# Inner sums over two slices, and stores that wait for GpSimd moved some slots back, in a masked graph attention kernel

## The chip, the cores and the metric

The kernel runs on one core of a Trainium2 chip. The metric is the device time of one execution in microseconds. A core has TensorE (matmuls, PE in the profile; its weight loads are PEld), VectorE (DVE), ScalarE (ACT), GpSimd (POOL) and SyncE (SP), whose queue issues nearly all DMAs of this kernel. Each engine works through its own instructions in their order, and so does SyncE's queue: an instruction that waits holds up all that stand behind it on its engine.

## What is computed

128 graphs of 128 nodes with 768 features go through one layer of attention with a normalization in front, 12 heads of 64, all in float32:

```python
h = jnp.maximum(_layernorm(x, axis=-1), 0.0)
q = _split_heads(h @ Wq + bq)
k = _split_heads(h @ Wk + bk)
v = _split_heads(h @ Wv + bv)
scores = jnp.einsum('bhqd,bhkd->bhqk', q, k) / jnp.sqrt(HD)
scores = scores + beta * adj_e
scores = jnp.where(adj_e > 0, scores, -9e15)
probs = jax.nn.softmax(scores, axis=-1)
x = x + einsum('bhqk,bhkd->bhqd', probs, v)   # heads put back together
```

The adjacency is non-zero in about one place of eight.

## The kernel before

**Groups and slices.** Four graphs make a group, and there are 32 groups. A group's projections come in three slices: `qk0` (queries and keys of heads 0 to 5), `v` (all heads), `qk1` (queries and keys of heads 6 to 11). A slice multiplies activations of 2 x 3 blocks (`A00` to `A12`) by weights of 3 x 3 blocks (`B00` to `B22`). Instead of 18 block products it takes the 15 of a fast scheme (`PRODUCTS`, line 66): sums of activation blocks (`S0` to `S14`, `SUMS_A`) meet sums of weight blocks (`T0` to `T13`, `SUMS_B`), and results are added up with signs.

**Two kinds of product.** `product` (line 564, slice `qk1`) takes a block product as it is, with its weight sums kept in SBUF. `product_z` (line 488, slices `qk0` and `v` from group 1 on) splits each block product once more in two by two and takes seven small products for eight. That needs four more subtractions or additions of 128x128 for each activation sum, made on GpSimd by `inner` (line 420) into `spbuf`, and a prepared weight tile of seven parts, of 448 KB. The 30 prepared tiles lie in DRAM (`kept`); `load_T` (line 298) brings them, one for each product, into a ring of five. A `product_z` issues the load of the tile five places on behind its own matmuls. GpSimd also undoes the scheme behind each finished result: `decode` (line 537).

**The first group.** The prepared tiles don't exist yet. Group 0 takes `qk0` and `v` by `plain_slice` (line 767), 18 units in which plain block products are added up in PSUM, while `prepare` (line 245) makes the 30 tiles step by step: sums on VectorE, four subtractions on GpSimd (`rest` or `finish`), then a store. Its `qk1` is taken with 15 products.

**Slots.** The order of the work is written out by hand. A slice has 15 slots (18 in `plain_slice`), one for each product. `then(at, f, ...)` puts a step into slot `at`, behind that product's matmuls and before its results are read out; `(at, "post")` puts it at the slot's end. `later(f, n)` puts off a step to the n-th slot's end from here on (1 is this one), over the slices' ends if need be; `overdue` runs those that are due. All engines get their instructions in this order.

**What runs beside the products** of group G: scores of heads 6 to 11 of the group before in `qk0` and of heads 0 to 5 of G in `v`, in slots 1 and 2; `attend` (probabilities times values, three in `qk0`, three in `qk1`), woven between the matmuls by `turn`; behind each of them `weigh` (quotients, VectorE and ScalarE), an addition to the input on GpSimd (`add`, line 661) and a store of 256 KB (`send`, line 664). For the groups to come: normalization and transposes in `v` and `qk1`, `sum_acts` (VectorE) and `inner` (GpSimd) of G + 1 in `qk1`, row statistics of G + 2 on VectorE (`row_stats`), whose moments (`row_moments`, line 383) are two small operations on GpSimd, a store to DRAM (line 395) and a load that spreads them over the partitions (line 396); the adjacency and x of G + 2 are loaded by SyncE too. `activations` (line 942) holds the slots of the sums; all but one of the sums and 14 of the 15 `inner` steps of G + 1 lie in `qk1` of G, in slots 3 to 14, the last ones in slots 0 and 1 of `qk0`.

Of the kernel before, what the change touches and what calls it, by code (L numbers as in the profile page):

```python
# [10 lines left out]
F32 = mybir.dt.float32  # L11
# [6 lines left out]
P = 128  # L18
# [96 lines left out]
def direct(ctx, tc, x, adj, wq, bq, wk, bk, wv, bv, beta, out, bad):  # L115
# [129 lines left out]
    def prepare(sl):  # L245
# [4 lines left out]
        def rest(n, t):  # L250
            e = nc.gpsimd
            e.tensor_tensor(t[:, 2], t[:, 4], t[:, 1], ALU.subtract)
# [16 lines left out]
        def finish(name):  # L269
            n = [i for i, p in enumerate(PRODUCTS) if p[1] == name][0]  # L270
            if name in made:
                rest(n, made[name])
            else:
                t, b = home(n), wt[sl, name]
                e = nc.gpsimd
                for z, c, i in ((0, 0, 0), (3, 1, 0), (4, 1, 1)):
                    nc.scalar.copy(t[:, z], b[:, c, i])
                e.tensor_tensor(t[:, 2], b[:, 1, 1], b[:, 0, 1], ALU.subtract)
                e.tensor_tensor(t[:, 6], b[:, 0, 1], b[:, 0, 0], ALU.subtract)
                e.tensor_tensor(t[:, 1], t[:, 4], t[:, 6], ALU.subtract)  # L280
                e.tensor_tensor(t[:, 5], t[:, 3], t[:, 1], ALU.subtract)
                k = kept[sl, n] = dram.tile([P, 7, P], F32, name=f"kept_{sl}_{n}")
                nc.sync.dma_start(k, t)
# [99 lines left out]
    def row_moments(G):  # L383
# [11 lines left out]
        nc.sync.dma_start(turned.rearrange("i b s -> b i s"), t.rearrange("p s g -> p (s g)"))  # L395
        nc.sync.dma_start(to.rearrange("p b s g -> p (b s g)"),
                          turned.rearrange("i b s -> i (b s)")[None].to_broadcast([NB, SQ, NB * 2 * GRP]))
# [245 lines left out]
    def attend_steps(G, oc):  # L643
# [24 lines left out]
        later(send, 3)  # L668
# [98 lines left out]
    def plain_slice(G, sl, todo):  # L767

        n = 0
        for r in range(2):  # L770
            for j in range(3):
# [3 lines left out]
                parts = (slice(0, N), slice(N, H2)) if sl != "v" and r == j == 0 else (slice(0, H2),)  # L775
                for at, k in [(at, k) for at in parts for k in range(3)]:
                    a, b = A[G, f"A{r}{k}"], wt[sl, f"B{k}{j}"]
                    for i in range(2):
                        for c in range(2):
                            lhs, rhs = b[:, c, i], a[:, c, at]  # L780
                            if sl == "v":
                                lhs, rhs = a[:, c, i * N:(i + 1) * N], b[:, c].rearrange("p i n -> p (i n)")
                            last = nc.tensor.matmul(p[:, i, at], lhs, rhs, start=(k == 0 and i == 0 and c == 0),
                                                    stop=(c == 1), skip_group_check=True)
# [20 lines left out]
                    for f in todo.get(n, ()):  # L805
                        f()
                    overdue()
                    n += 1
# [133 lines left out]
    def activations(G, first):  # L942

        for name, at in (("A01", 3), ("A00", 5), ("A02", 6), ("A11", 9), ("A10", 17), ("A12", 24)):
            if at >= 15:
                then(at - 15, to_hT, G, int(name[1]), int(name[2]))
            elif first:
                then(0, to_hT, G, int(name[1]), int(name[2]))
# [6 lines left out]
    raw_qk(1, const.tile([P, NC * VH * 2], F32, name="wqk1"), ((0, 3),))  # L955
# [10 lines left out]
    for r in range(2):  # L966
        then(6, load_x, 1, r)
    for n in range(len(SUMS_A)):
        then(n + 5, after, sum_acts, 0, n)
# [235 lines left out]
```

## Time and profile before

| what | us |
|---|---|
| median of 2 runs (3175.19 to 3183.41) | 3179.3 |
| the profiled execution | 3173.59 |
| its span, first to last instruction | 3171.8 |
| VectorE's waits for the adjacency (`adjT`, 30 times) | 273.8 |
| matmuls of `product_z` on T_qk with spbuf, busy | 707.0 |
| the same on T_v with spbuf, busy | 648.5 |
| GpSimd's additions of results (`xo`, 189) | 242.0 |

The mean granted clock of TensorE is 0.946. A row of the groups of instructions names line, engine, operation, what it writes and reads, shapes and count; then the busy time, the mean of one in ns, the idle time of the engine in front of them and what ended most of it. A row of the waits has who waited for whom, the sum in us, how often, and the longest. A row of the timeline has start, length, engine, line, operation, tiles, how many were merged into it, and in brackets the idle time before it with its releaser. A row of the windows has the stretch, its length, then for PE, PEld, DVE, ACT and POOL the busy time and the number of instructions, then the granted clock, the DMA engines' busy share and GB/s. Lines that are helpers' (L501, L577, L662) hold all products or additions of their kind.

### The profile page before, as it was taken

How to read it: one execution, taken by the hardware profiler on the slowest of the kernel's cores; microseconds unless marked ns; L12 is line 12 of the kernel's file. 1: busy time of each engine (PE TensorE's matmuls, PEld its weight loads, DVE VectorE, ACT ScalarE, POOL GpSimd, SP SyncE). 2: the span in 40 equal slices, each digit the busy share in tenths (PEclk: the TensorE clock that was granted, in tenths of full speed). 3: DMA queues.
4: the chain of work that ended last, by engine and by line, in shares of the span. 5: the costliest groups of instructions: out<-in, count | busy, mean ns of one | idle time of the engine just before them, and what ended most of it. 6: DMA issues, size and time to landing. Idle time of an engine off the chain costs nothing.

```text
span 3171.8 us, 113085 instructions
## 1 busy us (share of the span) xinstructions
PE 2807.9 (89%) x46385; PEld 2452.2 (77%) x46385; DVE 2163.9 (68%) x4755; ACT 1341.2 (42%) x3999; POOL 2323.2 (73%) x4146
## 2 busy tenths in 40 slices
PE   7888889888889888898888898888988888988898
PEld 6677778787778777787887787777877777877787
DVE  4677667667677666676676776666766667766665
ACT  1344344444344443444443444444444434444343
POOL 4967778667787678786777777687867777767773
PEclk8899999999999999999999999999999999999999
DMA  8486667776667776667766677666677666876654
GB/s 213 144 251 206 200 194 211 242 221 198 194 188 247 230 205 208 194 208 242 224 200 196 187 244 235 206 206 193 201 242 226 197 199 188 240 234 210 199 178 132
DMA packets 526215, 660.86 MB, mean 208 GB/s; under 512 B 105460, under 2 KB 401664, under 8 KB 525696
## 3 DMA queue, kind: packets, MB, share of 16 engines
q1 hardware_dynamic: 525368, 653.20, 68.5%
q8 instruction: 367, 6.01, 0.8%
q14 instruction: 152, 1.25, 0.1%
q10 hardware_dynamic: 328, 0.40, 0.1%
HBM read 589.26 MB, written 64.21 MB: 206 GB/s over the span
## 4 chain that ended last, share of the span: by engine, by line


## 5 line engine op out<-in xcount | busy, mean ns | idle before, releaser
L501 PE MATMUL bank<-spbuf,T_qk 128*64 128x128 f32 x7440 | 707.0, 285 | 0.9 <-issue 0.9
L501 PE MATMUL bank<-S,T_qk 128*64 128x128 f32 x4092 | 443.5, 292 | 289.5 <-DMA T_qk<-kept_qk 288.7
L501 PE MATMUL bank<-T_v,spbuf 128*64 128x128 f32 x7440 | 648.5, 273 | 1.3 <-issue 1.3
L636 ACT ACTIVATE o<-bank,sm 128x64 f32<-128x64 f32 x1524 | 354.5, 315 | 643.7 <-DVE sm L630 433.0
L501 PEld LDWEIGHTS bank<-S,T_qk 128*64 128x64 f32 x4092 | 280.4, 148 | 306.3 <-issue 295.0
L652 PEld LDWEIGHTS bank<-v,e 128*64 128x64 f32 x6048 | 420.2, 137 | 110.0 <-ACT o L636 0.5
L501 PEld LDWEIGHTS bank<-spbuf,T_qk 128*64 128x64 f32 x7440 | 484.6, 146 | 1.0 <-issue 1.0
L501 PEld LDWEIGHTS bank<-T_v,spbuf 128*64 128x64 f32 x7440 | 459.4, 137 | 1.4 <-issue 1.4
L652 PE MATMUL bank<-v,e 128*64 128x65 f32 x6048 | 441.6, 221 | 0.3 <-ACT o L636 0.3
L501 PE MATMUL bank<-T_v,S 128*64 128x128 f32 x4092 | 405.2, 275 | 18.6 <-ACT v L515 14.7
L546 POOL TENSOR_TENSOR qk<-qk 128x256 f32<-128x256 f32 x186 | 135.9, 731 | 378.9 <-DVE qk L527 378.9
L577 PE MATMUL bank<-S,wqk 128*64 128x256 f32 x3072 | 402.4, 380 | 0.0
L587 ACT ACTIVATE qk<-bank,bqk 128x256 f32<-128x256 f32 x384 | 158.6, 476 | 570.8 <-PE bank L577 433.8
L527 DVE TENSOR_TENSOR qk<-qk,bank 128x512 f32<-128x512 f32 x310 | 209.4, 675 | 161.8 <-PE bank L501 159.1
L527 DVE TENSOR_TENSOR v<-v,bank 128x512 f32<-128x512 f32 x310 | 212.1, 684 | 154.4 <-PE bank L501 97.6
L577 PE MATMUL bank<-S,qk_T 128*64 128x256 f32 x2560 | 317.1, 381 | 0.0
L557 POOL TENSOR_TENSOR v<-v 128x128 f32<-128x128 f32 x186 | 85.8, 461 | 270.9 <-DVE v L527 201.4
L501 PEld LDWEIGHTS bank<-T_v,S 128*64 128x64 f32 x4092 | 259.5, 137 | 31.9 <-ACT v L515 21.7
L619 DVE SCALAR_TENSOR_TENSOR e<-bank,biasT 128x512 f32<-128x512 f32 x378 | 237.0, 681 | 50.7 <-PE bank L615 50.6
L520 ACT ACTIVATE qk<-bank,bqk 128x128 f32<-128x128 f32 x186 | 67.7, 364 | 438.5 <-PE bank L501 379.0
L662 POOL TENSOR_TENSOR xo<-xo,o 128x512 f32<-128x512 f32 x189 | 242.0, 1280 | 11.8 <-ACT o L636 11.6
L622 ACT ACTIVATE e<-e 128x512 f32<-128x512 f32 x378 | 223.8, 633 | 8.9 <-DVE e L619 8.8
(166 smaller groups left out, 6081.1 us busy)
## 6 DMA issues: line engine op xcount, KB each, us to landing
T_qk<-kept_qk SPq DMA_DIRECT2D x465, 448.0 KB, 5.1
T_v<-kept_v SPq DMA_DIRECT2D x465, 448.0 KB, 4.4
x<-in_x_dram SPq DMA_DIRECT2D x254, 192.0 KB, 4.7
xo<-in_x_dram SPq DMA_DIRECT2D x189, 256.0 KB, 5.5
out_dram<-xo SPq DMA_DIRECT2D x189, 256.0 KB, 4.1
half<-in_x_dram SPq DMA_DIRECT2D x232, 192.0 KB, 4.8
adj<-in_adj_dram SPq DMA_DIRECT2D x128, 64.0 KB, 2.1
kept_qk<-prep_qk SPq DMA_DIRECT2D x15, 448.0 KB, 2.9
```

The costliest lines, as they stand in the source:

```text
L501: nc.tensor.matmul(p[z // 4][q:q + HD, z % 4, :], lhs[:, q:q + HD], rhs, start=(first and z % 4 == 0), stop=True, skip_group_check=True)
L520: nc.scalar.activation(t[:, 0], p[0][:, 0], AF.Identity, bias=bqk[:, 0, oc:oc + 1], scale=float(sign))
L527: nc.vector.tensor_tensor(t[:, 0:4], t[:, 0:4], p[0], op)
L546: e.tensor_tensor(t[:, 1:4:2], t[:, 1:4:2], twice(0), ALU.add)
L557: e.tensor_tensor(v[:, 0:2, 0:HD], heads(0), heads(3), ALU.add)
L577: nc.tensor.matmul(p[q:q + HD, i, :], lhs[:, q:q + HD], rhs, start=(first and i == 0 and c == 0), stop=(c == 1), skip_group_check=True)
L587: opened[0] = nc.scalar.activation(t[:, i, :], p[:, i, :], AF.Identity, bias=bqk[:, i, oc:oc + 1], scale=float(sign))
L619: taken[0] = nc.vector.scalar_tensor_tensor(e, ps[oc, i].rearrange("p (g n) -> p g n", g=GRP), SCORE_CAP * ISCALE, biasT[G], op0=ALU.min, ...
L622: nc.scalar.activation(e, e, AF.Exp, scale=1.0 / ISCALE)
L636: nc.scalar.activation(o[:, b], pa[:, b, 0:HD], AF.Copy, scale=t[:, 1, b:b + 1])
L652: nc.tensor.matmul(pa[q:q + HD, 2 * g + i, :], es[G, oc, i][:, 2 * r + g, q:q + HD], vt[G, "v", r, h // 4][:, 4 * g + h % 4, :], start=Tru ...
L662: nc.gpsimd.tensor_add(t, t, o.rearrange("p a (b j) d -> p (a b) (j d)", j=2))
```

## The change

- **Steady groups, sums.** Of the 15 `inner` steps of group G + 1, nine stay in slice `qk1` of G (slots 6 to 14) and six go to slots 0 to 5 of the next `qk0`. They now stand in the order in which the products use them. The slots of the activation sums stay.
- **Steady groups, queue of SyncE.** The store of the row moments is put off by `later(..., 5)`, the load behind it by `later(..., 8)`; `send` goes from `later(..., 3)` to `later(..., 6)`. `row_moments` itself moves from slot 14 to 13, the row statistics (with the loads of half rows) from slots 1, 4, 8, 12 to 2, 5, 8, 11.
- **First group, third slice.** `qk1` of group 0 goes by `plain_slice`, row block 1 first. Group 0 needs no activation sums any more; the weight sums of `qk1` move, five into that slice and ten into slice `v` of group 1. Sums and `inner` steps for group 1 are divided over `qk1` of group 0 and `qk0` of group 1.
- **Preparation.** Two of the four subtractions of each prepared tile go from GpSimd to VectorE. The steps are spread over three slices instead of two. The raw weights of `qk1` are loaded from slot 8 of the first slice, not ahead of it; x of group 1 from slot 5, not 6.

```diff
-        def rest(n, t):
-            e = nc.gpsimd
-            e.tensor_tensor(t[:, 2], t[:, 4], t[:, 1], ALU.subtract)
-            e.tensor_tensor(t[:, 6], t[:, 1], t[:, 0], ALU.subtract)
-            e.tensor_tensor(t[:, 1], t[:, 4], t[:, 6], ALU.subtract)
-            e.tensor_tensor(t[:, 5], t[:, 3], t[:, 1], ALU.subtract)
+        def rest(n, t, b11, b12, b22):
+            nc.vector.tensor_tensor(t[:, 6], b12, b11, ALU.subtract)
+            nc.vector.tensor_tensor(t[:, 2], b22, b12, ALU.subtract)
+            nc.gpsimd.tensor_tensor(t[:, 1], t[:, 4], t[:, 6], ALU.subtract)
+            nc.gpsimd.tensor_tensor(t[:, 5], t[:, 3], t[:, 1], ALU.subtract)
...
-        nc.sync.dma_start(turned.rearrange("i b s -> b i s"), t.rearrange("p s g -> p (s g)"))
-        nc.sync.dma_start(to.rearrange("p b s g -> p (b s g)"),
-                          turned.rearrange("i b s -> i (b s)")[None].to_broadcast([NB, SQ, NB * 2 * GRP]))
+        later(lambda: nc.sync.dma_start(turned.rearrange("i b s -> b i s"), t.rearrange("p s g -> p (s g)")), 5)
+        later(lambda: nc.sync.dma_start(to.rearrange("p b s g -> p (b s g)"),
+                                        turned.rearrange("i b s -> i (b s)")[None].to_broadcast([NB, SQ, NB * 2 * GRP])), 8)
...
-        later(send, 3)
+        later(send, 6)
...
-    def plain_slice(G, sl, todo):
+    def plain_slice(G, sl, todo, rows=(0, 1)):
...
+                            for q in range(0, P, HD) if sl == "qk1" else (slice(0, P),):
+                                q = slice(q, q + HD) if sl == "qk1" else q
+                                last = nc.tensor.matmul(p[q, i, at], lhs[:, q], rhs, start=(k == 0 and i == 0 and c == 0),
+                                                        stop=(c == 1), skip_group_check=True)
+                            turn()
...
-    def activations(G, first):
-
-        for name, at in (("A01", 3), ("A00", 5), ("A02", 6), ("A11", 9), ("A10", 17), ("A12", 24)):
...
-        for n, at in enumerate((2, 10, 3, 5, 6, 7, 11, 12, 13, 14)):
-            then(at, sum_acts, G, n)
-        for n, at in ((0, 3), (1, 3), (2, 4), (11, 4), (12, 5), (4, 6), (5, 7), (6, 8), (8, 10), (3, 11), (7, 12), (9, 13),
-                      (10, 14), (13, 14)):
-            then(at, inner, G, n)
...
+    def activations(G):
+
+        at_slots(to_hT, G, ((2, ("A10",)), (9, ("A12",))))
+        at_slots(sum_acts, G, ((2, (0,)), (3, (2,)), (5, (3,)), (6, (4,)), (7, (5,)), (10, (1,)), (11, (6,)), (12, (7,)),
+                               (13, (8,)), (14, (9,))))
+        at_slots(inner, G, ((6, (0,)), (7, (4,)), (8, (2,)), (9, (1,)), (10, (8,)), (11, (6,)), (12, (5,)), (13, (3,)),
+                            (14, (10,))))
+
+    def rest_of_activations(G):
+        at_slots(sum_acts, G, ((0, (10,)),))
+        at_slots(inner, G, ((0, (7,)), (1, (13,)), (2, (9,)), (3, (11,)), (4, (12,)), (5, (14,))))
...
-    for n in range(len(SUMS_A)):
-        then(n + 5, after, sum_acts, 0, n)
+    then(8, lambda: raw_qk(1, const.tile([P, NC * VH * 2], F32, name="wqk1"), ((0, 3),)))
...
-        then(g, stats, 1, g)
-        then(10 + 2 * g, norm, 1, g)
-    then(6, lambda: mom.extend(moments_1(1, 0, GRP * NB)))
-    then(8, lambda: moments_2(1, 0, GRP * NB, *mom))
-    for n in range(len(SUMS_B)):
-        then(n + 3, sum_weights, "qk1", n)
+        then(2 * g, stats, 1, g)
+        then(12 + g, norm, 1, g)
+    then(8, lambda: mom.extend(moments_1(1, 0, GRP * NB)))
+    then(10, lambda: moments_2(1, 0, GRP * NB, *mom))
     for n in range(18):
-        then(n, step, 2)
-    bias(0, 4, 9, 12, 16)
+        then(n, step, 1 + (n % 3 == 1))
+    bias(0, 9, 11, 14, 16)
     plain_slice(0, "v", todo)
-    step(len(prep))
...
-    slice_of(0, "qk1", todo)
+    plain_slice(0, "qk1", todo, (1, 0))
...
-        then(0, sum_acts, G, 10)
-        then(1, inner, G, 14)
+        if G > 1:
+            rest_of_activations(G)
...
+                for at, n in enumerate((3, 4, 5, 6, 7, 8, 9, 10, 13, 14)):
+                    then(at + 3, sum_weights, "qk1", n)
...
-            for g, at in enumerate((1, 4, 8, 12)):
+            for g, at in enumerate((2, 5, 8, 11)):
...
-            then(14, row_moments, G + 2)
+            then(13, row_moments, G + 2)
             then(14, add_raw, G + 2)
```

More of the change, by code (lines that the diff above doesn't have):

```diff
@@ L765, in slice_z @@
         run([product_z(G, sl, n) for n in ZORDER], todo)
-    def plain_slice(G, sl, todo):
+    def plain_slice(G, sl, todo, rows=(0, 1)):
         n = 0
-        for r in range(2):
+        for r in rows:
             for j in range(3):
@@ L773, in plain_slice @@
                 p = bank.rearrange("p (i w) -> p i w", i=2)
[L775 removed]
+                parts = (slice(0, N), slice(N, H2)) if sl == "qk0" and r == j == 0 else (slice(0, H2),)
                 for at, k in [(at, k) for at in parts for k in range(3)]:
@@ L806, in plain_slice @@
                         f()
+                    while weighing:
+                        weighing.popleft()()
                     overdue()
+                    for f in todo.get((n, "post"), ()):
+                        f()
                     n += 1
```

46 lines of the change are left out of this document (24 added, 22 removed).

## The prediction

> **What bounds the kernel now.** I read the page's totals and its costliest groups first, for the engine and the wait that matter.
>
> ```profile
> span 3171.8 us, 113085 instructions
> ...
> PE 2807.9 (89%) x46385; PEld 2452.2 (77%) x46385; DVE 2163.9 (68%) x4755; ACT 1341.2 (42%) x3999; POOL 2323.2 (73%) x4146
> ...
> L501 PE MATMUL bank<-S,T_qk 128*64 128x128 f32 x4092 | 443.5, 292 | 289.5 <-DMA T_qk<-kept_qk 288.7
> ```
>
> TensorE is the bound, and of its 364 us outside busy time (3171.8 - 2807.9) one wait holds 289: products of the first slice of a group wait for a prepared weight tile T_qk to land. The list of the DMA queue's own waits says why the tile is late.
>
> ```profile
> SPq L665 <- POOL spbuf L424: 295.1, 32, 24.1
> SPq L395 <- POOL row L392: 242.1, 29, 8.4
> ```
>
> SyncE's queue stands for 537 us behind GpSimd: before stores of results (L665) and before the row moments' small store (L395). Both are issued in order with the T loads. One group in order of time, SyncE's queue and then TensorE:
>
> ```profile
> 1515.84 0.41 SPq L665 DMA_DIRECT2D out_dram<-xo  x1
> 1524.69 0.55 SPq L395 DMA_DIRECT2D turned<-row  x1
> ...
> 1527.26 2.02 SPq L434 DMA_DIRECT2D adj<-in_adj_dram  x4
> 1529.38 0.43 SPq L303 DMA_DIRECT2D T_qk<-kept_qk  x1
> ```
>
> ```profile
> 253.46 0.39 PE L501 MATMUL bank<-S,T_qk 128*64 128x128 f32 x4
> ...
> 1512.84 0.39 PE L501 MATMUL bank<-S,T_qk 128*64 128x128 f32 x4
> ...
> 1523.50 0.39 PE L501 MATMUL bank<-spbuf,T_qk 128*64 128x128 f32 x4
> 1533.48 0.69 PE L501 MATMUL bank<-S,T_qk 128*64 128x128 f32 x4 [9.59 <-DMA T_qk<-kept_qk]
> ...
> 1537.55 0.40 PE L501 MATMUL bank<-S,T_qk 128*64 128x128 f32 x4
> ...
> 1553.45 0.40 PE L501 MATMUL bank<-T_v,S 128*64 128x128 f32 x4
> ...
> 1580.76 0.81 PE L577 MATMUL bank<-S,qk_T 128*64 128x256 f32 x5
> ...
> 1609.46 0.42 PE L501 MATMUL bank<-S,T_qk 128*64 128x128 f32 x4
> ...
> 3062.89 0.39 PE L501 MATMUL bank<-S,T_qk 128*64 128x128 f32 x4
> ...
> 3078.60 0.44 PE L501 MATMUL bank<-S,T_qk 128*64 128x128 f32 x4 [3.12 <-DMA T_qk<-kept_qk]
> ...
> 3095.18 0.42 PE L501 MATMUL bank<-T_v,S 128*64 128x128 f32 x4
> ```
>
> TensorE starts group 16's first slice at 1512.84 and has used its five tiles by 1523.9. The sixth could be asked for after product 0, near 1515, but is issued at 1529.38 behind the moments' store (which waited for GpSimd until 1524.7) and four adjacency loads. The rows also give the lengths: this group's slices take 40.6 (to 1553.45), 27.3 (to 1580.76) and 28.7 us (to 1609.46). From 253.46 to 3062.89 there are 29 groups of 96.88 us, so the first slice takes 96.88 - 27.3 - 28.7 = 40.9 us on the average. The last group has no moments ahead of it; its first slice takes 3095.18 - 3062.89 - 3.12 = 29.2 us outside its one wait. That slice also lacks the mask's steps on VectorE, which I take as hidden in the others too, VectorE being busy 68%. A clean slice is thus 11.7 us shorter: a wait of some 9.6, and some 2 that follow it, since the four matmul records of a step take 0.69 us after the wait and 0.40 again from 1537.55.
>
> The Trainium skill (TensorE: Matmul & The Clock Gate, "What's actually happening") says that an idle window of about 3.4 us halves the array's clock and that about 3.4 us of work restore it. By that rule the trace agrees with the 0.69, and the wait of 3.12 (0.44 after it) stayed below the limit; new waits of 1 or 2 us would by it cost only themselves, and one of 4 some 2 more.
>
> **The change in the steady groups.** The moments' store goes from slot 14 of the third slice to the next slice's slot 2, its reload to slot 5; a result's store comes three slots later, so the last two of the third slice fall behind T loads; the adjacency load stays in slot 14 with no wait ahead of it. What they waited for must now be early enough, and that is GpSimd's queue.
>
> ```profile
> 1524.46 0.20 POOL L392 TENSOR_TENSOR row<-meanrow,row 128x4 f32<-128x4 f32 x1
> ...
> 1527.58 0.53 POOL L445 MEMSET biasT<- 128x512 f32 x1
> 1540.35 0.73 POOL L546 TENSOR_TENSOR qk<-qk 128x256 f32<-128x256 f32 x1 [12.24 <-DVE qk L527]
> ...
> 1560.45 0.73 POOL L549 TENSOR_TENSOR qk<-qk 128x256 f32<-128x256 f32 x1
> 1569.70 0.46 POOL L557 TENSOR_TENSOR v<-v 128x128 f32<-128x128 f32 x1 [8.52 <-DVE v L527]
> ...
> 1588.24 0.46 POOL L562 TENSOR_TENSOR v<-v 128x128 f32<-128x128 f32 x1
> ```
>
> ```profile
> 1596.21 0.93 ACT L636 ACTIVATE o<-bank,sm 128x64 f32<-128x64 f32 x4 [0.53 <-DVE sm L630]
> ```
>
> GpSimd has three blocks of unbroken work: the v decodes, 1569.70 to 1588.70, 19.0 us; then 15 inner sums, three adds, the moments and a memset, from 7.9 us into the third slice to 15.3 into the next (1528.11 - 1512.84): 28.7 - 7.9 + 15.3 = 36.1 us; then six decodes of qk with three adds, 1540.35 to 1561.18, 20.8 us. The second block holds about 2.0 us for each inner sum ((36.1 - 3 x 1.3 - 1.2 - 0.5)/15, with some 1.3 for an add).
>
> The change puts nine inner sums in the third slice and six in the next, in the order in which they are used. The moments then stand behind eight sums and two adds, not 14 sums and two adds. From 7.9 us: three sums to 13.9; the first add waits for its quotient, ready at 1597.14, 16.4 us into the slice, so 2.5 us of idleness are new; add to 17.7, three sums to 23.7, add to 25.0, two sums to 29.0, moments to 30.2. That is 1.5 us into the next slice. Five products and the scores take 11.1 us there (1512.84 to 1523.9), so slot 2 ends near 6.5 and the store no longer waits, nor do the result stores in slots 0 and 3. T loads go out from slot 0. The 9.6 and the 2 go.
>
> What is late next is the qk decode. The six remaining inner sums stand ahead of it, and none may wait long: their activation sums are at their old slots. The first decode can begin 16.1 us into a clean slice (1540.35 - 1512.84 less 11.4, this slice's excess over 29.2). Without the new idleness the second block ends at 15.3, in time; with all of it at 17.8, 1.7 us late. The decodes then end 20.8 later, between 7.7 and 9.4 us into the second slice, where scores want the last of them:
>
> ```profile
> 1561.24 0.45 PE L615 MATMUL bank<-qk 64*64 64x128 f32 x8 [0.15 <-POOL qk L549]
> ```
>
> Today they are served 7.7 us into the slice (1561.18 - 1553.45), with a wait of 0.15. So 0 to 1.8 us of a new TensorE wait; I take 1.1, nearer to the end with the idleness, as half of it may be won back by sums that run beside less VectorE work. For T loads at the clean pace, the issues with their size and time to landing, and a stretch of the last group:
>
> ```profile
> T_qk<-kept_qk SPq DMA_DIRECT2D x465, 448.0 KB, 5.1
> ...
> xo<-in_x_dram SPq DMA_DIRECT2D x189, 256.0 KB, 5.5
> ```
>
> ```profile
> 3078.60:3095.20 16.60, 16.60 (x349) 16.60 (x351) 11.34 (x31) 5.95 (x24) 12.21 (x17) 1.00 0.99 337
> ```
>
> In the last group's clean stretch the DMA engines carried 337 GB/s at 0.99 busy and TensorE waited for nothing; fifteen tiles of 448 KB and six results or inputs of 256 KB in 29.2 us are 290 GB/s. I take 0.4 us for what may still come late, between 0 and 2. Stores sent later free the three xo buffers later: a load that reuses one comes six slots behind its store, some 9 us, against 5.5 for a landing, so nothing is charged. The row statistics and the half loads issued beside them move by a slot (1, 4, 8, 12 to 2, 5, 8, 11); three slots of 1.9 us (28.7/15) still cover a landing of 5.1, so nothing again, and some 1 us of VectorE's time where they don't. Saved: 11.7 - 1.1 - 0.4 = 10.2 us a group, 29 x 10.2 = 296 us.
>
> **The change in the first groups.**
>
> ```profile
> 101.40:150.80 49.40, 35.84 (x437) 24.46 (x438) 37.77 (x69) 21.53 (x59) 43.93 (x78) 0.83 0.35 121
> 150.60:193.40 42.80, 34.07 (x624) 31.80 (x621) 26.74 (x68) 15.51 (x49) 26.92 (x44) 0.92 1.03 269
> 193.40:224.90 31.50, 27.67 (x524) 25.51 (x522) 24.89 (x57) 16.97 (x43) 20.41 (x34) 1.00 0.71 231
> ```
>
> ```profile
> PE bank L338 <- DVE st L327: 10.8, 1, 10.8
> ...
> PE bank L615 <- DVE v L795: 13.6, 2, 10.3
> ```
>
> ```profile
> L252 POOL TENSOR_TENSOR prep_qk<-prep_qk 128x128 f32<-128x128 f32 x11 | 9.1, 831 | 12.8 <-DVE prep_qk L225 12.8
> ...
> L516 DVE TENSOR_TENSOR v<-bv_b,bank 128x128 f32<-128x128 f32 x186 | 52.7, 283 | 21.5 <-PE bank L501 20.7 <-ACT v L515 0.6
> ```
>
> TensorE waits 10.8 and 13.6 us in group 0, both for VectorE. Thirty tiles give two subtractions each from GpSimd to VectorE: up to 60 x 0.83 = 50 us less there, some 60 x 0.28 = 17 us more here (no row has this operation on VectorE from SBUF alone; it should lie between nothing and 30). Against that, VectorE loses 11 activation sums of group 0, and its 15 weight sums leave the v slice, which is where it was late. With the slow matmuls behind, the waits cost about 28; I take 19 of it back (5 to 28). The plain third slice has 18 units for 15 products: 3/15 of at most 28.7, which holds attention too, so 5.2 more (up to 5.7). Group 1's first slice falls from 42.8 to 31, as its transposed A00 and its sums come in just ahead of use: 11.8 less (8 to 13). Its v slice takes ten weight sums of under 1 us on a VectorE that was busy 24.9 of 31.5: 3 more (0 to 6). Together 19 - 5.2 + 11.8 - 3 = 22.6 less, from 2 to 36. The last group's 3.1 goes too, as its store moves; I count 2.
>
> **Sum.** 296 + 23 + 2 = 321 off the profiled execution's 3173.6 (span 3171.8 and some 2 around it) is 2853. The median shown, 3179.3, is 5.7 higher; the forecast is 2858.
>
> **Rivals.** *GpSimd takes over.* Its blocks of 75.9 us plus 2.5 leave 7 us in a period of 85, and any delay lands at the scores. For it: decodes already end within 0.15 us of their use. Against it: two pauses a group, 12.2 and 8.5 us, are there to use up. If sums wait for VectorE by 3 us more, TensorE waits about 4.5, and by slow matmuls as at 1533.48 loses 6: 5.3 a group saved, 154 + 25, about 3000. *T loads fall short.* DMA at 0.99 has nothing over; two waits of 1 us a group: 58 us back, 2916. *It doesn't do what it says.* If GpSimd's moments came as late as now, 11.8 us into the slice (1524.66), the store in slot 2 would hold the T loads of slots 3 and 4 until then; they would land from 16.9 on, bunched, for products due from 16.5 (11.1 and three of 1.8): some 2.5 us a group, 2930. This bounds it well, since the loads of slots 0 to 2 are out before. *Slower:* contention between GpSimd and VectorE.
>
> ```profile
> 1510.68 0.93 DVE L417 TENSOR_TENSOR S<-A,A 128x512 f32<-128x512 f32 x1
> ...
> 1511.02 0.90 POOL L426 TENSOR_TENSOR spbuf<-A 128x128 f32<-128x128 f32 x1
> ```
>
> A GpSimd subtraction takes 0.90 beside a VectorE sum and 0.46 alone (as L562 above). The same VectorE work squeezed into fewer us meets more of it. If all four steps of every inner sum took 0.90, a sum would take 3.6 for 2.0, GpSimd's chain 75.9 + 2.5 + 15 x 1.6 = 102.4 us, and with its pause of 8.5 for v 111 a group: 14 more than 96.9, 29 x 14 = 406, less 25 in the ends, about 3560. It decides from 10 us more, six or seven of the 15 sums at that rate (75.9 + 2.5 + 8.5 + 10 = 96.9). Against it: VectorE has only eleven such sums a group.
>
> The Trainium skill (GPSIMD Engine Reference, "Specifications") names that mechanism: the SBUF interfaces are shared, with contention from VectorE instructions with two SBUF inputs. By that rule, which the 0.90 bears out, the 60 moved subtractions would also slow GpSimd while they run.
>
> **How the numbers follow.** Forecast 0.72; GpSimd takes over 0.13; T loads 0.06; not as it says 0.05; slower 0.04. By the ends of its terms together (0 or 3.8 of new waits a group, 36 or 2 in the first groups) the forecast reaches from 2801 to 2946. From 2805 to 2940 lie nearly all of it, the T loads and the third case: 8 in 10, with the first rival left out above. A measurement of this kernel tells some 2% (64 us) from no change. Every case but the last is below 3116, though the third could fail in a way that I don't see: faster 0.93, within 2% 0.04, slower 0.03.
>
> **What would show it.** T_qk waits of TensorE near nothing; first slices of 29 to 31 us; the store of the moments issued between T loads with no wait on L392; GpSimd's pause before qk decodes gone, with a wait of about 1 us at L615 for L549; granted clock near 1.0. Wrong would be T_qk waits at another product, first slices above 33 us, or second slices that grow by over 3.

## The result, and the profile after

The changed kernel takes 2958.6 us (median of 2957.3 and 2959.89) against 3179.3: a ratio of 0.931, with a 95% interval of 0.925 to 0.936. It is clearly faster, and the time lies 101 us above the forecast and 19 above the range. The page of the profile after, its totals and the group of matmuls that held the old wait:

```profile
span 2955.5 us, 113446 instructions
...
PE 2784.0 (94%) x46433; PEld 2431.7 (82%) x46433; DVE 2131.3 (72%) x4794; ACT 1351.1 (46%) x3999; POOL 2287.8 (77%) x4086
...
L495 PE MATMUL bank<-S,T_qk 128*64 128x128 f32 x4092 | 414.9, 282 | 109.7 <-ACT qk L515 106.3
```

TensorE's busy share rose from 89 to 94%. The group that waited 288.7 us for T_qk waits 106.3 us now, and for something else: for ScalarE, which reads the qk banks out. The waits of all engines, sorted by their sums (who waited, for whom, us in total, times, longest):

```profile
ACT adjT L445 <- DVE biasT L444: 144.7, 31, 7.4
DVE biasT L444 <- POOL biasT L439: 126.5, 29, 4.4
...
PE bank L495 <- ACT qk L515: 106.3, 29, 3.7
...
PE bank L332 <- DVE st L321: 11.7, 1, 11.7
...
PE bank L609 <- POOL qk L543: 6.0, 19, 0.4
...
PE bank L495 <- DMA T_qk<-kept_qk: 3.8, 3, 1.8
```

The wait for T_qk is gone (3.8 us). Three waits, of 29 to 31 times each, stand in a row instead: TensorE for ScalarE, ScalarE for VectorE, VectorE for GpSimd's memset of the bias tile. SyncE's queue, in its own list of waits, has 26 us before the stores of results for GpSimd's additions and 23 for its inner sums, and 6 before the moments' store. In the kernel before these rows had 165, 295 and 242 us; the prediction counted only the last two of them:

```profile
SPq L659 <- POOL xo L656: 26.1, 5, 20.1
SPq L659 <- POOL spbuf L418: 23.2, 7, 16.0
...
SPq L389 <- POOL spbuf L421: 6.3, 27, 0.3
```

One group in order of time, all engines, with the first matmul of group 2's and the last group's first slice ahead and behind (start, length, engine, line, what; in brackets the idle time before and its releaser):

```profile
237.54 0.39 PE L495 MATMUL bank<-S,T_qk 128*64 128x128 f32 x4
...
1497.89 0.39 PE L495 MATMUL bank<-S,T_qk 128*64 128x128 f32 x4
...
1500.36 0.20 POOL L386 TENSOR_TENSOR row<-meanrow,row 128x4 f32<-128x4 f32 x1
...
1505.16 0.56 SPq L389 DMA_DIRECT2D turned<-row  x1
...
1514.18 0.45 POOL L421 TENSOR_TENSOR spbuf<-S,spbuf 128x128 f32<-128x128 f32 x1
1514.58 0.52 POOL L439 MEMSET biasT<- 128x512 f32 x1
1515.13 0.73 DVE L444 COPY_PREDICATED biasT<-kp,adjT 128x512 f32<-128x512 uint8 x1 [4.37 <-POOL biasT L439]
...
1515.90 0.63 ACT L445 ACTIVATE adjT<-adjT 128x512 f32<-128x512 f32 x1 [4.74 <-DVE biasT L444]
1516.43 0.35 ACT L514 ACTIVATE qk<-bank,bqk 128x128 f32<-128x128 f32 x1
1516.68 0.48 ACT L515 ACTIVATE qk<-bank 128x384 f32<-128x384 f32 x1
...
1517.22 0.44 PE L495 MATMUL bank<-S,T_qk 128*64 128x128 f32 x4 [3.69 <-ACT qk L515]
...
1519.75 0.65 PE L495 MATMUL bank<-S,T_qk 128*64 128x128 f32 x4
...
1522.46 0.39 PE L495 MATMUL bank<-S,T_qk 128*64 128x128 f32 x4
...
2852.62 0.39 PE L495 MATMUL bank<-S,T_qk 128*64 128x128 f32 x4
```

The moments end 2.7 us into the slice (1500.56 - 1497.89), and their store goes out between T loads with next to no wait. GpSimd's last inner sum ends near 1514.6, and only then comes its memset. VectorE has stood 4.37 us for it with the predicated copy; the square on ScalarE has stood 4.74 us for the copy, because it overwrites the tile that the copy reads; the readouts L514 to L517 stand behind the square on ScalarE, and TensorE, which finds no free bank, stands 3.69 us from 1513.53 on. After it the matmul steps of four take 0.65 us for a while, then 0.39 again.

From 237.54 to 2852.62 are 29 groups of 90.18 us; before they were 96.88. The slices, from the first matmul of one to that of the next in the timelines (means of the steady groups), for this kernel and those of the next section:

| kernel | us | first slice | v | third |
|---|---|---|---|---|
| before | 3179.3 | 40.9 | 27.3 | 28.7 |
| the change | 2958.6 | 34.1 | 27.3 | 28.7 |
| e1 memset ahead of the last three sums | 2836.8 | 29.2 | 28.1 | 28.7 |
| e2 square one step later | 2874.5 | 30.4 | 28.2 | 28.7 |
| e3 before, with the change of the queue alone | 2911.5 | 32.0 | 27.4 | 28.7 |
| e4 the change without that of the queue | 2935.7 | 33.0 | 27.7 | 28.7 |
| e5 memset ahead of the last sum alone | 2903.0 | 32.4 | 27.2 | 28.7 |
| e6 preparation back on GpSimd | 2965.9 | 34.4 | 27.3 | 28.7 |
| e7 e1, three additions later | 2828.8 | 29.1 | 28.0 | 28.7 |
| e8 e7, other slots in the first groups | 2833.3 | 29.1 | 28.1 | 28.7 |
| e11 e3, memset on VectorE | 2880.9 | 31.4 | 27.2 | 28.7 |
| e12 the change, memset on VectorE | 2835.0 | 29.2 | 28.1 | 28.7 |

Where the time went, of the spans' difference of 216.3 us (3171.8 - 2955.5): 29 x 6.7 = 194.4 in the steady groups, 15.9 in the first two (253.46 - 237.54), 6.0 at the end (108.9 - 102.9 from the last group's start).

### The profile page after: what moved, and what is told of

Its sections match the earlier page's. It is cut to its first block, busy times and chain, and to the rows that moved or that the text cites. A ratio compares the mean times of both kernels' runs of the same rounds, so it can differ in the third digit from the quotient of the medians.

```text
span 2955.5 us, 113446 instructions
## 1 busy us (share of the span) xinstructions
PE 2784.0 (94%) x46433; PEld 2431.7 (82%) x46433; DVE 2131.3 (72%) x4794; ACT 1351.1 (46%) x3999; POOL 2287.8 (77%) x4086
## 4 chain that ended last, share of the span: by engine, by line
## 5 line engine op out<-in xcount | busy, mean ns | idle before, releaser
L495 PE MATMUL bank<-spbuf,T_qk 128*64 128x128 f32 x7440 | 673.3, 278 | 0.2 <-issue 0.2
L646 PEld LDWEIGHTS bank<-v,e 128*64 128x64 f32 x6048 | 434.8, 144 | 107.5 <-ACT o L630 0.2
L495 PE MATMUL bank<-S,T_qk 128*64 128x128 f32 x4092 | 414.9, 282 | 109.7 <-ACT qk L515 106.3
L646 PE MATMUL bank<-v,e 128*64 128x65 f32 x6048 | 449.4, 228 | 0.0
L495 PEld LDWEIGHTS bank<-spbuf,T_qk 128*64 128x64 f32 x7440 | 445.4, 141 | 0.5 <-issue 0.5
L495 PE MATMUL bank<-T_v,S 128*64 128x128 f32 x4092 | 402.8, 275 | 17.5 <-ACT v L509 15.6
L571 PE MATMUL bank<-S,wqk 128*64 128x256 f32 x2976 | 389.5, 380 | 0.0
L495 PEld LDWEIGHTS bank<-S,T_qk 128*64 128x64 f32 x4092 | 252.9, 142 | 127.0 <-ACT qk L515 113.5
L571 PE MATMUL bank<-S,qk_T 128*64 128x256 f32 x2480 | 305.6, 379 | 0.0
L587 DVE TENSOR_TENSOR qk<-qk,bank 128x512 f32<-128x512 f32 (+1 forms) x311 | 208.2, 670 | 47.3 <-PE bank L571 34.0
L616 ACT ACTIVATE e<-e 128x512 f32<-128x512 f32 x378 | 227.3, 629 | 17.8 <-DVE e L613 17.3
L540 POOL TENSOR_TENSOR qk<-qk 128x256 f32<-128x256 f32 x186 | 135.7, 730 | 106.3 <-DVE qk L521 58.4
```

The source lines that it names most:

```text
L495: nc.tensor.matmul(p[z // 4][q:q + HD, z % 4, :], lhs[:, q:q + HD], rhs, start=(first and z % 4 == 0), stop=True, skip_group_check=True)
L540: e.tensor_tensor(t[:, 1:4:2], t[:, 1:4:2], twice(0), ALU.add)
L571: nc.tensor.matmul(p[q:q + HD, i, :], lhs[:, q:q + HD], rhs, start=(first and i == 0 and c == 0), stop=(c == 1), skip_group_check=True)
L587: added[G] = nc.vector.tensor_tensor(t[:, :, cols], t[:, :, cols], p[:, :, cols], ALU.add if sign > 0 else ALU.subtract)
L616: nc.scalar.activation(e, e, AF.Exp, scale=1.0 / ISCALE)
L646: nc.tensor.matmul(pa[q:q + HD, 2 * g + i, :], es[G, oc, i][:, 2 * r + g, q:q + HD], vt[G, "v", r, h // 4][:, 4 * g + h % 4, :], start=Tru ...
```

## The experiments

e1 to e8 are single executions; the kernel before took 3172.7 beside e1 to e4 and 3180.5 beside e5 to e8. e9 to e12 are medians of four.

**The chain from the memset.** e1 makes the memset two slots earlier and registers the bias steps ahead of the sums, so that three of the six sums stand behind it and not before; VectorE's and ScalarE's steps stay in their slots.

```diff
-        yield
+        if G < 3:
+            yield
         t = biasT[G] = work.tile([P, GRP, N], F32, tag="biasT", name=f"biasT_{G}", bufs=2)
         nc.gpsimd.memset(t, MASKED)
+        if G >= 3:
+            yield
...
         if G > 1:
+            if more:
+                bias(G + 1, 3, 5, 6, 12)
             rest_of_activations(G)
...
-        elif more:
-            bias(G + 1, 3, 5, 6, 12)
```

> The changed kernel with one memset moved: in groups 2 to 30 GpSimd clears the mask tile in slot 3 of the first slice, ahead of three of the six inner sums, not in slot 5 behind all six. Theory (chain through the mask: the memset ends behind the inner sums, VectorE's predicated copy waits for it, ScalarE's square waits for the copy, ScalarE's readout of the next products stands behind the square, TensorE waits for the bank): the wait of 3.7 us a group for ScalarE at L495 goes, and the slow matmuls behind it; first slices of 34.2 become 29.5 to 31, 29 x 3.2 to 4.7 us less, total 2820 to 2866. Rival (GpSimd is simply late with everything, decodes too): the wait moves to the scores of the second slice, which grow by 2 or more; total 2900 to 2940. Rival (ScalarE is overloaded in this slice): no change, 2950 to 2965.

2836.8 us. The timeline of one of its groups, whose first slice starts at 1525.43:

```profile
1536.37 0.52 POOL L440 MEMSET biasT<- 128x512 f32 x1
...
1538.30 0.82 DVE L447 COPY_PREDICATED biasT<-kp,adjT 128x512 f32<-128x512 uint8 x1
...
1539.15 0.63 ACT L448 ACTIVATE adjT<-adjT 128x512 f32<-128x512 f32 x1 [0.45 <-DVE biasT L447]
...
1539.68 0.35 ACT L517 ACTIVATE qk<-bank,bqk 128x128 f32<-128x128 f32 x1
```

The memset comes 10.9 us into the slice instead of 16.7, the copy waits for nothing, and the first slice takes 29.2 us: TensorE runs through. Its list of waits is headed by

```profile
PE bank L612 <- POOL qk L546: 20.6, 58, 0.4
```

which is the wait at the scores for the last decodes that the prediction had put at 1.1 us a group; 20.6 us are 0.7 a group, and the v slice is 0.8 longer than in the changed kernel, so it is near that size.

e2 leaves the memset where it is and sends the square one step later, off the readouts' way.

```diff
         nc.vector.copy_predicated(t, kp, a)
+        if G >= 3:
+            yield
         nc.scalar.activation(a, a, AF.Square, scale=1.0005 * math.sqrt(SUM_CAP) / (BIAS_CAP * ISCALE))
...
-            bias(G + 1, 3, 5, 6, 12)
+            bias(G + 1, 3, 5, 6, 9, 12)
```

> The changed kernel with one ScalarE operation moved: in groups 3 to 31 of the mask the square of the adjacency goes from slot 6 of the first slice to slot 9; memset and predicated copy stay. Theory (TensorE waits because ScalarE, in order, stands at the square): ScalarE's readouts no longer stand behind it, so the wait at L495 for ScalarE falls from 3.7 to 0 to 1 us a group; VectorE still waits 4.4 us for the memset, and its own readouts are late by that, which may cost TensorE up to 2. Total 2830 to 2890. Rival (VectorE's wait for the memset is what counts, whichever engine is named): the wait of 3 to 4 us stays and VectorE is named for it; 2940 to 2965.

2874.5 us. From its list of waits:

```profile
DVE biasT L444 <- POOL biasT L439: 127.3, 29, 4.8
...
PE bank L497 <- DVE qk L523: 25.8, 59, 0.9
```

VectorE waits for the memset as long as in the changed kernel (126.5), and most of the loss is gone all the same: ScalarE's place in the chain carried it. What is left comes over VectorE itself, whose additions L523 stand behind the copy.

e12 takes the memset off GpSimd altogether and leaves the order as it is.

```diff
-        nc.gpsimd.memset(t, MASKED)
+        nc.vector.memset(t, MASKED)
```

> The whole change with the memset of the bias on VectorE, at its old place in the order of the work. It cuts the same chain as e1 by another way. Theory (the chain from GpSimd's memset is what the changed kernel waits for): TensorE's wait for ScalarE's qk readouts falls from 106 us to under 10, 2830 to 2855, within 15 us of e1. Rival (e1 gained by the new place of the bias steps ahead of the sums, not by the memset): over 2900.

2835.0 us, a ratio to the kernel before of 0.892 (0.891 to 0.894). No wait for ScalarE's qk readouts is left among TensorE's larger ones; the first is again

```profile
PE bank L609 <- POOL qk L543: 20.4, 58, 0.4
```

Two cuts of the chain in different ways give the same time, so what e1 gained was the memset, not the place of the other steps.

**The two halves of the change.** e3 is the kernel before with the deferrals of the queue alone; e4 is the changed kernel with those undone.

```diff
-        nc.sync.dma_start(turned.rearrange("i b s -> b i s"), t.rearrange("p s g -> p (s g)"))
+        later(lambda: nc.sync.dma_start(turned.rearrange("i b s -> b i s"), t.rearrange("p s g -> p (s g)")), 5)
...
-        later(send, 3)
+        later(send, 6)
```

> The kernel before with the queue's part of the change alone: the store of the moments five slots later, its reload eight, result stores at six for three; sums and the first group as before. Theory (what held SyncE's queue is the order of issue, and it needs only the stores to stand behind T loads): the wait for T_qk falls from 9.2 us a group to 0 to 2, but GpSimd's block still ends 15.3 us into the slice with the memset last, so the mask's chain makes TensorE wait 1 to 4 us; first slices 31 to 34, total 2900 to 2990. Rival (the split of the sums is needed too, since the store in the next slice still finds GpSimd late): T_qk waits of 4 or more stay, total 3020 to 3120.

> The changed kernel with the queue's part undone: the moments' store and reload issued at once, result stores at three slots; the split of the sums, the first group and the preparation as changed. Theory (the moments now end 2.7 us into the first slice, so SyncE is held to about 5 by the store and its reload and to 7 by nothing else, the sixth tile lands near 11): T_qk waits of 0 to 3 us a group beside or in place of the wait for ScalarE, total 2955 to 3030. Rival (the deferral carries the gain by itself): T_qk waits come back to over 6, total above 3080.

2911.5 and 2935.7 us: each half alone beats the two together (2958.6). e3 came within its theory's range, e4 19 us below its own. One group of e3, whose first slice starts at 1486.05, in its timeline:

```profile
1501.15 0.52 POOL L445 MEMSET biasT<- 128x512 f32 x1
...
1501.71 0.73 DVE L450 COPY_PREDICATED biasT<-kp,adjT 128x512 f32<-128x512 uint8 x1 [2.17 <-POOL biasT L445]
1502.47 0.63 ACT L451 ACTIVATE adjT<-adjT 128x512 f32<-128x512 f32 x1 [3.15 <-DVE biasT L450]
...
1503.79 0.44 PE L501 MATMUL bank<-S,T_qk 128*64 128x128 f32 x4 [2.10 <-ACT qk L521]
```

The chain was in the old order too: its memset ends 15.6 us into the slice, in the kernel before 15.3 (1528.11 - 1512.84). There TensorE stood for T_qk until 1533.48, so that nothing was late. Take that stop away and the chain shows, with 1.8 to 3.0 us. Move the sums as well and the memset ends 17.2 us into the slice and the wait is 3.7: GpSimd has the same work in front of the memset, but its additions of results now wait for ScalarE's quotients, 57.0 us in all against 12.5 in e3, some 1.5 a group. e4 has part of both, in TensorE's waits:

```profile
PE bank L495 <- DMA T_qk<-kept_qk: 50.8, 50, 2.0
PE bank L495 <- ACT qk L515: 41.2, 28, 2.7
```

e11 asks whether the sums need to be moved at all: e3 with the memset on VectorE, the same edit as in e12.

```diff
-        nc.gpsimd.memset(t, MASKED)
+        nc.vector.memset(t, MASKED)
```

> The kernel before with the change's deferrals in SyncE's queue and nothing else of it (2911.5), now with the memset of the bias made by VectorE instead of GpSimd, so that the predicated copy waits for no GpSimd sum. Theory A (the split of the sums over two slices gains nothing by itself: once the bias chain is cut, putting off the stores is enough): the wait of ScalarE's readouts, 61 us, and the slow matmuls behind it go, 29 x 2.7 = 79 us less, 2820 to 2850, with first slices near 29.5. Theory B (the split is needed as well, since without it GpSimd's moments and qk decodes come late): waits for T_qk or at the scores of 1 us a group or more appear, 2865 to 2915.

2880.9 us, a ratio of 0.907 (0.905 to 0.909): 46 us behind e12. SyncE's and TensorE's lists of waits:

```profile
SPq L665 <- POOL spbuf L424: 201.3, 34, 24.1
...
SPq L665 <- POOL xo L662: 153.3, 68, 21.6
```

```profile
PE bank L501 <- DMA T_qk<-kept_qk: 31.7, 32, 3.3
PE bank L501 <- ACT qk L521: 16.9, 29, 1.1
```

Without the split the result stores still hold SyncE for 354 us (201.3 + 153.3; 459.8 in the kernel before), T loads among what stands behind, and the first slice is 2.2 us longer than in e12, as theory B had it. So the steady part of the change is needed beside the deferrals; in the changed kernel the memset hid its worth. Between the profiled executions of e11 and e12 lie 48 us: 29 x 1.28 = 37 in the steady groups (the v slice is 0.9 shorter in e11) and 11 in the start, where e11 lacks the changes of the first groups (group 2 begins at 248.3 there and at 237.2 in e12). e11 also lacks the moves of `row_moments` and the row statistics by a slot, so the 37 us belong to these and the split together; no run has the split alone.

**How the loss grows with the wait.** e5 lets only the last of the six sums go behind the memset.

```diff
-        at_slots(inner, G, ((0, (7,)), (1, (13,)), (2, (9,)), (3, (11,)), (4, (12,)), (5, (14,))))
+        at_slots(inner, G, ((0, (7,)), (1, (13,)), (2, (9,)), (3, (11,)), (4, (12,))))
...
             bias(G + 1, 3, 5, 6, 12)
+        if G > 1:
+            at_slots(inner, G, ((5, (14,)),))
```

> The changed kernel with the memset one inner sum earlier on GpSimd: in slot 5 ahead of the last of the six inner sums, not behind it. The chain through the mask then ends some 1.8 us earlier. Theory (that chain, and a wait of 3.7 us is long enough to slow the matmuls behind it while one of 1.9 isn't): the wait for ScalarE at L495 is 1.8 to 2.0 us a group and no slow matmuls follow; first slices 31.0 to 31.4, granted clock above 0.99, total 2862 to 2878, which is more than the 29 x 1.8 = 52 us of the wait itself. Rival (the slowing doesn't hang on the length of the wait): first slices 32.4, total 2900 to 2912. Rival (another wait stands right behind the first): first slices above 33, total above 2920.

2903.0 us. The wait fell by 1.6 us, to 2.1, but 20 of the 29 first slices fell to 32.9 and only 9 to some 31.3: the time is what the first rival gave. TensorE in two of its groups, 2.1 us of wait in both, and the windows of the same two slices:

```profile
2375.29 0.44 PE L495 MATMUL bank<-S,T_qk 128*64 128x128 f32 x4 [2.10 <-ACT qk L515]
...
2377.43 0.65 PE L495 MATMUL bank<-S,T_qk 128*64 128x128 f32 x4
...
2463.87 0.44 PE L495 MATMUL bank<-S,T_qk 128*64 128x128 f32 x4 [2.12 <-ACT qk L515]
...
2465.60 0.39 PE L495 MATMUL bank<-S,T_qk 128*64 128x128 f32 x4
```

```profile
2357.54:2390.47 32.93, 30.83 (x614) 29.89 (x612) 23.15 (x53) 17.19 (x56) 29.50 (x53) 0.95 0.73 225
2446.12:2477.42 31.30, 29.18 (x614) 28.26 (x612) 23.24 (x51) 16.84 (x54) 29.05 (x52) 1.00 0.77 238
```

The same work and the same wait, with a granted clock (third column from the end) of 0.95 in the one and 1.00 in the other, 1.6 us apart. What tells them apart is in the last section.

**The first groups.** e6 gives GpSimd its two subtractions of the preparation back.

```diff
-            nc.vector.tensor_tensor(t[:, 6], b12, b11, ALU.subtract)
-            nc.vector.tensor_tensor(t[:, 2], b22, b12, ALU.subtract)
+            nc.gpsimd.tensor_tensor(t[:, 6], b12, b11, ALU.subtract)
+            nc.gpsimd.tensor_tensor(t[:, 2], b22, b12, ALU.subtract)
```

> The changed kernel with the preparation's two moved subtractions back on GpSimd, 60 operations of 128x128; all else as changed. Theory of the prediction (it counted on 50 us less for GpSimd and 17 more for VectorE in the first groups, where TensorE waits for VectorE): the first groups become 3 to 12 us longer, total 2961 to 2971; steady groups the same. Rival (tiles wait for ScalarE's copies and for TensorE's readouts, not for GpSimd): within 2 us of the changed kernel's first groups.

2965.9 us. Group 2 starts at 239.9 instead of 237.5, between theory and rival. In the seven other runs with these first groups it starts between 235.8 and 238.4, so sharing the preparation is worth some 1.5 to 4 us, by a single execution. The other 5 are in the steady groups, which e6 doesn't touch, and nothing is built on them.

e7 puts the additions of the first three results one slot later in e1, to fill GpSimd's pauses, and e8 then moves group 1's moments and normalization, and four of its weight sums, to other slots.

```diff
-        later(add, 2)
+        later(add, 3 if oc < 3 else 2)
...
-        then(12 + g, norm, 1, g)
-    then(8, lambda: mom.extend(moments_1(1, 0, GRP * NB)))
-    then(10, lambda: moments_2(1, 0, GRP * NB, *mom))
+        then(16 + g // 2, norm, 1, g)
+    then(13, lambda: mom.extend(moments_1(1, 0, GRP * NB)))
+    then(15, lambda: moments_2(1, 0, GRP * NB, *mom))
...
+            for at, n in enumerate((3, 4, 5, 6)):
+                then(9 + at, sum_weights, "qk1", n)
...
-                for at, n in enumerate((3, 4, 5, 6, 7, 8, 9, 10, 13, 14)):
+                for at, n in enumerate((7, 8, 9, 10, 13, 14)):
                     then(at + 3, sum_weights, "qk1", n)
```

> The run with the early memset (2836.8 us), and in the third slice GpSimd's additions one slot later, each behind one inner sum more. Theory (GpSimd stands idle some 2 us a group for the first quotient, all its later work comes later by that, and the scores of the second slice wait for the last decode by 0.9 us): second slices of 28.1 become 27.2 to 27.5, total 2808 to 2820. Rival (the decodes are bound by VectorE's readouts, not by GpSimd's queue): no change, 2832 to 2840. Rival (ScalarE's quotients wait for the additions, two buffers of results): slower, above 2842.

> The run before it, and in the first groups: the column moments of group 1 in slots 13 and 15 of group 0's second slice, not 8 and 10; four of ten weight sums in group 1's first slice, not its second. Theory (TensorE waits 11.5 us at the moments since VectorE is behind, and group 1's second slice is long because VectorE has ten sums more there): the moments' wait falls below 5, the second slice of 37 becomes 33 to 35, together 6 to 14 us less than the run before it. Rival (VectorE's lag only moves to the readouts of the same slices): within 3 us of it.

2828.8 and 2833.3 us. In e7 GpSimd's wait for the quotients fell from 53.8 to 11.9 us, but the v slice stayed at 28.0 and the wait at the scores at 20.4 us, so the theory of e7 failed: that idleness isn't what the scores wait for. In e8 TensorE's wait at the moments falls to 3.3 us, and the lag is elsewhere. Group 1's first slice and its v slice took 35.3 and 37.1 us in e7; in e8 the windows are

```profile
135.80:175.00 39.20, 32.32 (x628) 30.19 (x626) 32.99 (x77) 16.89 (x55) 31.16 (x52) 0.96 0.89 252
175.00:208.90 33.90, 29.27 (x519) 26.68 (x515) 28.70 (x63) 16.86 (x43) 21.31 (x33) 0.95 0.73 224
```

These windows begin and end 0.4 to 0.7 us behind the slices; from first matmul to first matmul the two took 39.0 and 33.8 us, 72.8 together against 72.4, and group 2 begins at 236.9 in both. VectorE is busy 61.7 of the 73.1 us (32.99 + 28.70), so sending its work from one of the two slices to the other gains nothing.

e9 and e10 are e7 and e1 again, with an interval. The texts below describe them loosely: in both the memset stands ahead of the last three of the six sums, and in e9 the additions are put off by one slot more.

> The kernel of e7 again, timed in rounds for an interval: the changed kernel with the memset ahead of the six sums and the additions of the first three results put off by fewer slots. Theory (the bias chain was the changed kernel's new wait, and nothing has taken its place): 2825 to 2835 us, 0.885 to 0.895 of the kernel before. Rival (the single look was a lucky one, the kernel is near the changed kernel's 2959): over 2880.

> The kernel of e1 again, timed in rounds: only the memset is moved ahead of the six sums. Theory: 2832 to 2842 us, about 0.892 of the kernel before, and 5 to 10 us above the run with the earlier additions. Rival (the earlier additions do nothing, the 8 us between the single looks were scatter): both within 3 us of each other.

2833.7 (2829.3 to 2834.1) and 2835.4 (2834.9 to 2837.5); ratios 0.8935 (0.892 to 0.895) and 0.8942 (0.893 to 0.896). The two intervals overlap, and e12 has the same time: the later additions gain 2 us at most, not the 5 to 10 that e10's theory gave. The best version is thus the change with the memset taken out of the way: 0.89 of the kernel before, where the changed kernel has 0.93.

## Why the prediction was wrong, point by point

**The bound and the wait that goes: right.** The T_qk wait fell from 288.7 to 3.8 us, and the moments are early enough: 2.7 us into the slice, forecast 1.5. The clean first slice of 29.2 us, read off the last group, is to the tenth what e1 and e12 reach; the changed kernel's own, 34.1, is past the 33 that the prediction named as a sign of being wrong.

**GpSimd's second block: right.** It ends 17.2 us into the slice (1515.10 - 1497.89), between the 15.3 and 17.8 of the prediction.

**"What is late next is the qk decode": the step that failed.** The prediction counted the memset as half a microsecond of that block and didn't ask who waits for its end. It saw that the last group, from which it read the clean slice, has no mask's steps, and put them at nothing in the other groups because VectorE is busy 68%. e1 and e12 show that VectorE's own work on them is indeed hidden (29.2 us with it); what isn't hidden is that it waits for GpSimd, and a share of busy time can't show that. The decode isn't the next user: the predicated copy is, then the square, then the readouts of the qk banks, and TensorE wants these 15.6 us into the slice (1513.53 - 1497.89), before the block ends. Its own block's end of 15.3 to 17.8, with two numbers of this profile, prices it: the copy of 0.73, the square of 0.63 and the first two readouts take 2.1 us from the memset's end to TensorE's start (1517.22 - 1515.10), and with TensorE there at 15.6 that is 1.8 to 4.3 us of wait. In the profile of before no row shows that wait, since TensorE's stop for T_qk covered it. It measured 106.3 us, and with the slow matmuls 4.9 us a group (34.1 - 29.2): 143 us, of which e1, e2 and e12 remove 84 to 124 in their times.

**The decode's own price: right, but not yet due.** In the changed kernel the 3.7 us of delay give GpSimd time, and the scores wait 6.0 us in all. When the chain is cut, 0.7 us a group appear there (20.6 us in e1, 20.4 in e12), and the v slice is 0.7 to 0.8 longer (forecast 1.1, 0 to 1.8). A cut chain and these terms together give 29 x (96.88 - 86.04) = 314 us in e1 (from its first slices of group 2 at 236.53 and of the last group at 2731.82), forecast 296.

**T loads: right.** 0.4 us a group was taken for late loads; 3.8 us in all came, and with the chain cut no more than that (4.3 in e1, 3.5 in e12).

**Slow matmuls behind a wait: wrong in its limit.** The prediction let waits of 1 or 2 us cost only themselves and one of 4 some 2 more. The 3.7 us cost 1.3 more on the mean, as forecast for such a wait, but in e5 the 2.1 us cost 1.7 more in most groups (counts in the last section). The Trainium skill (TensorE: Matmul & The Clock Gate, "What's actually happening") puts the limit at an idle window of about 3.4 us; here 2.05 to 2.15 was mostly enough, and the measurement decides. The last section has the limit that all traces here show.

**The first groups: 15.9 against 22.6.** Of TensorE's two waits for VectorE, that of 13.6 us is gone. That of 10.8 us, for group 1's statistics, is still there with 11.7. It is 7.7 to 11.8 us in the other runs with these slots, 7.7 with the subtractions back on GpSimd (e6) as in one run without (e9), so it doesn't hang on the subtractions; only in e8, with the moments five slots later, is it 3.3. Windows of the third slice of group 0 and the next two of the changed kernel:

```profile
99.10:135.95 36.85, 36.85 (x481) 26.03 (x482) 27.27 (x60) 13.29 (x39) 24.68 (x45) 1.00 0.58 189
135.95:171.55 35.60, 31.03 (x626) 28.52 (x624) 29.42 (x71) 16.82 (x53) 31.39 (x53) 1.00 0.95 268
171.55:208.85 37.30, 30.73 (x522) 28.27 (x523) 32.05 (x68) 17.14 (x43) 23.37 (x34) 0.91 0.67 207
```

The third slice of group 0 took 49.2 us before (101.35 to 150.59), with the 13.6 us of wait and slow matmuls in it. The plain one runs unbroken at full clock and still takes 36.9 us, 8.2 more than the later third slices of 28.7 (forecast 5.2 for its three units). Group 1's first slice gave 7.2 (forecast 11.8), its v slice took 5.9 (forecast 3), VectorE being busy 32 of 37 us there. The end gave 6.0, forecast 2.

**The rivals.** GpSimd did remain the engine that sets the end, as the rival at 3000 had it, but at another place: not at the scores but at the readouts, over two engines that are each less busy than it. Contention was no matter: the four steps of the inner sums take 0.52 us on the mean, before and after (341 sums each). The total: 101 us of 29 x 10.2 didn't come (194 for 296), the first groups fell short by 7, the end gave 4 more.

## What to carry to other kernels

When a long wait goes, list all that ends during that wait, and for each, who is behind it in order on the other engines; the profile of before shows no wait for such a chain while a longer one covers it. A small instruction at the end of a long block (a memset of 0.5 us) has the block's lateness, and where its user shares an in-order engine with readouts, the matmuls get it. Two halves of a change can each be good and be worse together, so try each alone, and the pair with the new wait cut.

## What was not expected of the hardware

TensorE's clock drops after short waits, in some groups and not in others. In each steady first slice of the changed kernel, e3, e5 and e6 TensorE waits once for ScalarE's readouts. Slow steps (four matmuls in 0.65 us) came after

| wait, us | slices with slow steps |
|---|---|
| 1.76 to 1.95 | 0 of 14 |
| 2.05 to 2.15 | 26 of 35 |
| 2.24 to 3.04 | 6 of 9 |
| 3.54 to 3.75 | 49 of 58 |

and cost nearly the same whatever the wait: the slice was 1.7 us longer on the mean than 29.1 plus its wait where they came, 0.2 or less where they didn't. The Trainium skill (TensorE: Matmul & The Clock Gate, "What's actually happening") also says that the window runs free of the program, and the traces agree. In each of them the granted clock changes only on a grid of 3.41 us steps that is fixed for the execution, and 78 of the 81 slow stretches counted above are one such window long: 3.41 us at half the clock lose 1.7. Windows on that grid, around the two waits of 2.1 us in e5 shown above:

```profile
2373.14:2376.55 3.41, 1.31 (x30) 1.26 (x30) 1.83 (x3) 1.80 (x5) 3.24 (x6) 1.00 1.06 371
2376.55:2379.96 3.41, 3.41 (x46) 3.41 (x44) 2.24 (x7) 0.93 (x4) 2.34 (x4) 0.50 0.51 155
...
2461.88:2465.30 3.42, 1.43 (x34) 1.43 (x36) 1.67 (x3) 1.80 (x5) 3.19 (x7) 1.00 0.97 340
2465.30:2468.71 3.41, 3.41 (x82) 3.41 (x78) 3.09 (x10) 1.70 (x8) 2.49 (x4) 1.00 0.66 211
```

The first wait lies in one window, which is idle for 2.10 us (3.41 - 1.31), and the next window has half the clock. The second wait begins 0.13 us before its window, which is idle for 1.99, and the clock stays. All fourteen traces, from group 2's start to the last group's, fall apart at one place: each of the 117 full-clock windows that a slow one follows has TensorE idle for 2.01 us or more, each of the 10,173 that a full one follows for 2.01 or less. So a wait under 2.0 us alone never cost clock here, and one of 3.7 escaped when a window's edge cut it in two. So did the 3.12 us in the last group of the kernel before, which the prediction took to be below a limit: an edge divides it into 1.23 and 1.89.
